# Projections of the first three batches as whole float32 matmuls in a planned transformer-block kernel

## The chip, the cores and the metric

The kernel runs on one core of a Trainium2 chip. A core has a matrix engine (TensorE, PE in the profile), a vector engine (VectorE, DVE), a scalar engine (ScalarE, ACT), a general engine (GpSimd, POOL) and a queue engine (SyncE, SP) that only issues transfers here. Each takes its instructions strictly in the order of its own queue and waits for the others through semaphores. PEld in the profile is TensorE loading stationary operands, which overlaps its matmuls. The metric is the time of one execution on the device in microseconds (us), the median over several runs.

## The reference, cut to what matters

For 16 batches of 512 tokens with 512 features, in float32:

```
n   = layernorm(x)                                    # no gain, no bias
h   = rmsnorm(n) * g_res @ W_in.T + b_in              # the projection, "a"
s   = scan over tokens of rmsnorm(ctx[:, :, :512]) * g_init   # decaying running sum
idx = clip(cumsum(boundary marks from mask) - 1)      # "plug": a row of s for each token
x   = x + h + s[idx]                                  # gather
y   = layernorm(x)
xr, xk = mix of y and y shifted by one token (mu_r, mu_k)
r   = sigmoid(xr @ W_r.T);  k = relu(xk @ W_k.T) ** 2
out = x + r * (k @ W_v.T)
```

So each batch has four matrix products of 512 x 512 x 512: a, k, r and v. The marks of a batch come from counting how many boundaries of the mask fall on each token; a running sum of the counts, cut at one, gives the index.

## The kernel before, in words

**Products in three passes.** A product in float32 is made of three products in the faster form fp32r: each operand is split into a high part (a copy to fp32r, `hi_w` for a weight) and a low part (the operand minus its high part, `lo_w`), and the list `QW` adds high by high, high by low and low by high. For one batch and 128 tokens that is 12 fp32r matmuls of 128 x 512, in three groups of four. The weights are kept whole in `wsa`, `wsk`, `wsr`, `wsv` (the transfers' target, two halves each) and split in `wha`, `wla` and so on.

**The projection.** Before the projection the weight W_in is scaled: `pm` (four plain float32 matmuls of 128 x 512 with `gmean`) makes the mean that the layernorm takes off, and `wsa<-wsa,small,pm` on VectorE folds gain and mean into the weight, a chunk at a time. Thus the raw x can be projected, and the scale of the norm (`rs`) is applied when the result `pa` is added to x (`a_end`). The operand has x with features on partitions. For batches 0 to 2 (`BY_PE`) x is loaded as it lies and turned by TensorE against the identity in `consts` into four buffers `tx` (`turn_x`); ScalarE copies each to its high part `xh` and VectorE makes the low part (`split_x`). For later batches a turned copy (`raw`) is loaded from memory. Batch 0 runs its projection chunk by chunk over four results at once (`a_first`), the others result by result (`a_mm`).

**The rest of a batch.** ScalarE squares the context rows `cx` and VectorE scales and scans them, with one carry product `pc` on TensorE; SP writes the scan to memory (`dr`); POOL gathers its rows by `plug` and adds them to x. VectorE takes the statistics, POOL a power, VectorE or ScalarE makes y; TensorE turns y (`tr`), ScalarE and VectorE mix it (`pv`, `m`), and k, r and v follow. `plugs(b0, n)` makes the index for batch 0 alone and then for groups of batches: `count` on TensorE, `marks` on VectorE, one matmul with `tri`, `index` on VectorE.

**The planner.** No line fixes the order of the instructions. Each piece of work is given with `add` (engines that may do it and a cost, what it reads and writes, a due time) and `Plan.order` deals the pieces to the engines by lateness, engine by engine; then each engine's queue stands fixed in that order. `START` and `PERIOD` set the order of TensorE's stages, `SHIFT` moves the due times of a stage by some microseconds, `ONLY` gives a stage's shared work to VectorE (0) or POOL (1), `ON_ACT`, `KR_DVE` and `Y_DVE` say which engine makes some statistics, squares and y, and `SLOTS` counts the buffers of each kind; `ps` and `tr` are eight banks of PSUM. `WARM` puts filler matmuls on `ones` (128 x 128) ahead of a stage, and `HEAT` at the start; their results are not used. Transfers from SP are tied to what TensorE is planned to have finished by then. `InOrder` records every operation at one line, L300, so that the profile's groups differ by tile.

Of the kernel before, what the change touches and what calls it, by code (L numbers as in the profile page):

```python
# [11 lines left out]
F32 = mybir.dt.float32  # L12
# [277 lines left out]
class InOrder:  # L290
# [27 lines left out]
PASS = 0.935  # L318
PERIOD = lambda i: (("a", i + 1), ("k", i))
TAT = {3: (0, 1, 2, 3)}  # L320
TAT_OF = {0: {0: (0, 1, 2, 3)}, 1: {0: (0, 1, 2, 3)}, 2: {0: (0, 1, 2, 3)}, 3: {0: (0, 1), 2: (2, 3)}, 4: {0: (0, 1), 2: (2, 3)}}
# [3 lines left out]
HEAT = 8  # L325
SHIFT = {
    ("a", 0): 2.1,
    ("gather", 0): 23.8,
    ("k", 0): 2.0,
    ("load", 0): -10.1,  # L330
    ("mix_k", 0): 5.2,
    ("mix_r", 0): -10.7,
    ("norm2", 0): -17.9,
    ("plugs", 0): -30.6,
    ("rv", 0): 1.3,
    ("scan", 0): -7.2,
    ("sq", 0): -19.5,
    ("stat1", 0): -7.7,
    ("store", 0): 1.6,
    ("wk", 0): -5.2,  # L340
    ("wv", 0): -6.2,
    ("a", 1): 10.4,
    ("bias", 1): 2.6,
    ("gather", 1): 3.0,
    ("k", 1): 4.0,
    ("mix_k", 1): -1.5,
    ("mix_r", 1): -3.9,
    ("norm2", 1): -3.6,
    ("plugs", 1): 0.3,
    ("rv", 1): 12.6,  # L350
    ("split_x", 1): -7.5,
    ("sq", 1): -9.3,
    ("stat1", 1): 0.2,
    ("a", 2): 1.0,
    ("bias", 2): 53.6,
    ("gather", 2): -18.5,
    ("load", 2): 5.1,
    ("mix_k", 2): 1.2,
    ("mix_r", 2): 4.1,
    ("norm2", 2): 6.6,  # L360
    ("rv", 2): -0.4,
    ("scan", 2): 0.4,
    ("split_x", 2): -5.3,
    ("sq", 2): 30.1,
    ("stat1", 2): -1.6,
    ("store", 2): -50.4,
    ("a", 3): 8.2,
    ("bias", 3): -12.0,
    ("gather", 3): -1.8,
    ("k", 3): -3.2,  # L370
    ("load", 3): -3.1,
    ("mix_r", 3): -1.7,
    ("norm2", 3): 10.1,
    ("split_x", 3): 9.0,
    ("sq", 3): 2.7,
    ("stat1", 3): -16.2,
    ("store", 3): 9.3,
    ("a", 4): 13.9,
    ("bias", 4): -18.4,
    ("gather", 4): 11.9,  # L380
    ("k", 4): 4.9,
    ("load", 4): 16.5,
    ("mix_k", 4): 0.0,
    ("mix_r", 4): -47.3,
    ("norm2", 4): -4.5,
    ("plugs", 4): 4.7,
    ("rv", 4): -2.0,
    ("split_x", 4): -0.3,
    ("sq", 4): 2.2,
    ("stat1", 4): 2.5,  # L390
    ("store", 4): -10.4,
# [3 lines left out]
ONLY = {  # L395
    ("rv", 0): 0,
    ("k", 2): 0,
    ("wr", 0): 0,
    ("k", 3): 1,
    ("mix_r", 0): 0,  # L400
    ("split_x", 3): 0,
    ("bias", 1): 0,
    ("wk", 0): 1,
    ("mix_r", 2): 0,
    ("rv", 3): 0,
    ("mix_k", 0): 1,
    ("wv", 0): 0,
    ("wv", 1): 0,
    ("mix_k", 3): 1,
    ("rv", 2): 0,  # L410
    ("wk", 3): 1,
    ("bias", 3): 0,
    ("wr", 2): 0,
    ("wr", 3): 1,
    ("mix_k", 2): 1,
    ("split_x", 2): 0,
    ("wv", 2): 0,
# [3 lines left out]
WARM = {  # L421
    ("k", 1, 0): 1,
    ("x", 2): 32,
    ("a", 3, 0): 15,
    ("r", 0, 0): 14,
    ("a", 2, 1): 7,
    ("a", 0, 0): 29,
    ("x", 0): 1,
    ("v", 0, 0): 10,
    ("x", 1): 1,  # L430
}
TIE = 5.0
KR_DVE = (1, 3, 4, 5, 10, 11, 15)
# [4 lines left out]
RAW_IN = {2: ("op", "raw")}  # L438
CX_IN = {}
NLATE = 4  # L440
NWHOLE = 2
Y_DVE = (0, 1, 2, 3)
# [5 lines left out]
LOADS = ["raw2"]  # L448
B_DUE, P_DUE = 3.31, 83.3
START = [("x", 0), ("a", 0), ("a", 1), ("x", 1), ("x", 2), ("a", 2), ("k", 0), ("t", 0)]  # L450
T0 = 14.3
ON_ACT = (0, 1, 3, 4, 5, 6, 9, 10, 11, 13, 15)
# [3 lines left out]
def block_kernel(  # L456
# [88 lines left out]
    LO = ((DVE, 0.61), (POOL, 1.26))  # L545

# [94 lines left out]

    def split_x(b, c):
        if b in BY_PE:
            n, t = f"xh{b}_{c}", f"tx{b}_{c}"
            add((ACT, 0.52), lambda e: e.copy(S[n][:, 0], S[t]), K(t, *J), K(n, 0), new={n: OP}, early=40)
            add((DVE, 0.6), lambda e: e.tensor_tensor(S[n][:, 1], S[t], S[n][:, 0].bitcast(F32), ALU.subtract),
                K(t, *J) + K(n, 0), K(n, 1))
            return
# [136 lines left out]

    def a_mm(b, j, due, kind=PS):
        n = f"pa{b}_{j}"
        sl = slice(j * P, (j + 1) * P)
        new = warm(("a", b, j), {n: kind}, due)
        for k, (q, w) in enumerate(QW):  # L790
# [8 lines left out]
    def a_first():  # L799

        ns = [f"pa0_{j}" for j in J]
        new = warm(("a", 0, 0), {n: TRP for n in ns}, due["a", 0, 0])
        for k, (q, w) in enumerate(QW):
# [217 lines left out]
    def plugs(b0, n):  # L1021
        cp = f"cp{b0}"
        cnt = lambda: S[cp][:, : n * NJ].rearrange("p (b j) -> p b j", j=NJ)
        pb = lambda: S[cp][:, n * NJ :]
        for b in range(b0, b0 + n):
# [7 lines left out]
            def count(e, b=b, oh=oh):  # L1033
# [5 lines left out]
                new=None if b > b0 else {cp: (("ps", "tr"), [P, n * (NJ + 1)], F32)})  # L1039

        def marks_1(e):

            bm = S[f"bm{b0}"] = spool.tile([P, 1, NJ], F16, tag="bm", name=f"bm{b0}")
            run = S[f"run{b0}"] = spool.tile([P, 1, NJ], F32, tag="pf", name=f"run{b0}")
            for j in J:
                if j:
                    e.tensor_scalar(run[:, 0, j : j + 1], cnt()[:, 0, j : j + 1], 1.0, run[:, 0, j - 1 : j], ALU.min, ALU.add)
                else:
                    e.tensor_scalar(run[:, 0, 0:1], cnt()[:, 0, 0:1], 1.0, None, ALU.min)
            e.tensor_copy(bm[:, 0, NJ - 1 : NJ], run[:, 0, NJ - 1 : NJ])  # L1050
# [27 lines left out]
    for what, b in START:  # L1078
        if b < NB and (what != "x" or b in BY_PE):
            for j in J:  # L1080
                slot((what, b, j), 0.43 if what in "tx" else 3 * PASS)
# [254 lines left out]
```

## Time and profile before

| what | value |
|---|---|
| median of 3 runs | 809.89 us (809.76 to 810.18) |
| the profiled execution's own time | 808.87 us |
| its span, first to last instruction | 807.1 us |
| mean granted TensorE clock | 0.994 |
| TensorE busy | 788.4 us (98%) |
| VectorE, ScalarE, GpSimd busy | 594.3, 486.0, 453.1 us |
| TensorE's first projection matmul | at 18.27 us |
| first matmul of r of batch 0 | at 83.96 us |
| moved by DMA | 134.69 MB, mean 167 GB/s |

A group of the profile reads: line, engine, operation, result<-operands (buffer numbers left out), sizes, count; then busy time and mean duration of one in ns; then the engine's idle time just before these instructions, with what ended most of it. In an answer in order of time the two first numbers are start and duration in us, and the bracket holds the idle time before and what ended it. Matmuls are pipelined, so the duration of one (about 400 ns) is longer than the time from one to the next; a group of four fp32r matmuls of 128 x 512 begins 0.93 us after the one before it. A plain float32 matmul stands as two records.

### The profile page before, as it was taken

The page shows a single profiled execution, that of the slowest core. Times are in us where ns is not written, and L with a number is a line of the kernel's source. Part 1 is how long each engine was busy: PE and PEld are TensorE (multiplying, and loading weights), DVE is VectorE, ACT ScalarE, POOL GpSimd, SP SyncE. Part 2 cuts the span into 40 slices and gives each one's busy share as a digit, 9 for nine tenths or more (in the row PEclk, how much of TensorE's full clock was granted, in tenths as well). Part 3 has the DMA queues.
Part 4 walks back from the last instruction along what each step waited for, and adds up shares of the span by engine and source line. Part 5 has one row for each costly group of instructions (what it writes and reads, how often), then busy time and mean ns, then how long its engine had stood idle before and what let it go on. Part 6 is the DMA issues. An engine that isn't in the chain of part 4 may idle for free. (4 is left out here: it accounts for less than half of the span.)

```text
span 807.1 us, 11158 instructions
## 1 busy us (share of the span) xinstructions
PE 788.4 (98%) x3627; PEld 628.2 (78%) x3627; DVE 594.3 (74%) x1323; ACT 486.0 (60%) x950; POOL 453.1 (56%) x374
## 2 busy tenths in 40 slices
PE   7998999999999999999999999999999999999997
PEld 4776877878787888888788888878788888888885
DVE  6899798989789696785857679685866949464432
ACT  6937496655483767467566756457675664655540
POOL 2843766574767656567665556537856554661220
PEclk8999999999999999999999999999999999999999
DMA  9867586895775777667665766756786674430011
GB/s 327 270 95 262 104 220 170 288 220 160 144 234 147 179 199 206 157 209 145 212 140 171 220 157 209 157 162 152 184 234 157 209 138 171 73 89 0 9 45 52
DMA packets 52554, 134.69 MB, mean 167 GB/s; under 512 B 4752, under 2 KB 5264, under 8 KB 50576
## 3 DMA queue, kind: packets, MB, share of 16 engines
q1 hardware_dynamic: 35744, 102.39, 37.3%
q0 software_dynamic: 16608, 31.46, 24.2%
q8 instruction: 28, 0.46, 0.2%
q14 instruction: 30, 0.25, 0.1%
q10 hardware_dynamic: 144, 0.13, 0.0%
HBM read 85.73 MB, written 33.55 MB: 148 GB/s over the span
## 5 line engine op out<-in xcount | busy, mean ns | idle before, releaser
L300 POOL TENSOR_TENSOR m<-pv,m 128x512 fp32r<-128x512 f32 x86 | 120.9, 1414 | 121.3 <-ACT m L300 59.7
L300 PE MATMUL pa<-wha,xh 128*128 128x512 f32 x512 | 136.7, 404 | 5.8 <-DVE x L300 2.0
L300 PE MATMUL pw<-whv,ka 128*128 128x512 f32 x512 | 139.0, 398 | 0.0
L300 POOL DMA_INDIRECT x<-dr,plug x64 | 113.2, 1769 | 45.3 <-issue 17.0
L300 PE MATMUL pr<-whr,m 128*128 128x512 f32 x512 | 138.4, 397 | 0.0
L300 PE MATMUL pk<-m,whk 128*128 128x512 f32 x512 | 133.8, 396 | 0.6 <-DVE x L300 0.6
L300 ACT ACTIVATE pv<-tr,om 128x384 f32<-128x384 f32 (+1 forms) x256 | 100.8, 485 | 52.4 <-PE tr L300 28.5
L300 DVE SCALAR_TENSOR_TENSOR pv<-tr,small,pv 128x511 f32<-128x511 f32 x128 | 94.9, 741 | 38.7 <-ACT pv L300 37.9
L300 PEld LDWEIGHTS pa<-wha,xh 128*128 128x128 f32 x512 | 96.9, 191 | 31.9 <-DVE x L300 2.8
L300 PEld LDWEIGHTS pk<-m,whk 128*128 128x128 f32 x512 | 95.6, 188 | 24.8 <-DVE x L300 1.0
L300 PEld LDWEIGHTS pr<-whr,m 128*128 128x128 f32 x512 | 95.5, 188 | 23.0 <-DVE kr L300 0.4
L300 PEld LDWEIGHTS pw<-whv,ka 128*128 128x128 f32 x512 | 95.0, 188 | 21.8
L300 ACT CAST m<-pv 128x512 fp32r<-128x512 f32 x128 | 76.1, 642 | 37.1 <-DVE pv L300 31.8
L300 ACT ACTIVATE sg<-pr 128x512 f32<-128x512 f32 x64 | 38.1, 598 | 95.6 <-PE pr L300 88.6
L300 DVE TENSOR_TENSOR ka<-kr,ka 128x512 fp32r<-128x512 f32 x48 | 35.9, 749 | 76.3 <-ACT ka L300 76.2
L300 DVE TENSOR_TENSOR sg<-pw,sg 128x512 f32<-128x512 f32 (+1 forms) x65 | 43.9, 676 | 41.5 <-PE pw L300 41.5
L300 ACT ACTIVATE junk<-cx 128x1024 bf16<-128x1024 f32 x64 | 67.5, 1055 | 6.7 <-DMA cx<-cx 6.1
L300 PE MATMUL pa<-wla,xh 128*128 128x512 f32 x256 | 71.2, 401 | 0.3 <-POOL wla L300 0.3
L300 ACT ACTIVATE y<-x,r 128x512 f32<-128x512 f32 x48 | 38.9, 814 | 53.7 <-DVE r L300 37.4
L300 PE MATMUL pw<-wlv,ka 128*128 128x512 f32 x256 | 70.4, 397 | 0.0
L300 PE MATMUL pr<-wlr,m 128*128 128x512 f32 x256 | 70.3, 396 | 0.0
L300 PE MATMUL pk<-m,wlk 128*128 128x512 f32 x256 | 69.9, 396 | 0.0
(116 smaller groups left out, 1238.9 us busy)
## 6 DMA issues: line engine op xcount, KB each, us to landing
cx<-cx SPq DMA_DIRECT2D x64, 512.0 KB
dr<-cx SPq DMA_DIRECT2D x64, 256.0 KB
out<-x SPq DMA_DIRECT2D x31, 512.0 KB
x<-x SPq DMA_DIRECT2D x15, 1024.0 KB
x<-bc POOLq DMA_DIRECT2D x14, 1024.0 KB
raw<-xT SPq DMA_DIRECT2D x26, 512.0 KB
wsa<-winT SPq DMA_DIRECT2D x2, 512.0 KB
x<-x SPq DMA_DIRECT2D x4, 256.0 KB
```

Of the source, the lines that this page charges most:

```text
L300: r = self._tc.keep_in_program_order(op(*args, **kwargs))
```

## The change

For batches 0 to 2 (`A_WHOLE`) the projection takes x and the scaled W_in unsplit, as plain float32 matmuls: four for each 128 tokens in place of twelve fp32r ones. Their turned x is copied out of PSUM once, to `xt` (ScalarE or VectorE), and not split. All batches' projections now go result by result (`ROWS_FIRST`). W_in is still split, for the batches from 3 on. The transfers at the start have a new order (`FIRST`): one part of batch 0's context, the small constants, x of batch 0, `consts`, W_in, then the other parts of the context with the bias and gain rows between; x, context of batch 1 follow ahead of x of batch 2 and W_k. The marks write only the last running sum to fp16, the running sum of each group is kept in float32, and the index is made inside the PSUM buffer `cp`, which grows for it, and written to `plug` by the operation that cuts it. The planner's settings (`SHIFT`, `ONLY`, `WARM`, `START` and others) have new values, and so each engine's order is new.

```diff
 PASS = 0.935
+WHOLE = 0.86
-TAT_OF = {0: {0: (0, 1, 2, 3)}, 1: {0: (0, 1, 2, 3)}, 2: {0: (0, 1, 2, 3)}, 3: {0: (0, 1), 2: (2, 3)}, 4: {0: (0, 1), 2: (2, 3)}}
+TAT_OF = {
+    0: {1: (0, 1), 3: (2, 3)},
+    2: {0: (0, 1, 2, 3)},
+    1: {1: (0, 1), 3: (2, 3)},
...
-HEAT = 8
+HEAT = 10
 SHIFT = {
...
 ONLY = {
...
+    ("bias", 0): 1,
+    ("bias", 1): 1,
...
-WARM = {
-    ("k", 1, 0): 1,
-    ("x", 2): 32,
-    ("a", 3, 0): 15,
-    ("r", 0, 0): 14,
-    ("a", 2, 1): 7,
-    ("a", 0, 0): 29,
-    ("x", 0): 1,
-    ("v", 0, 0): 10,
-    ("x", 1): 1,
-}
+WARM = {("r", 0, 0): 7, ("x", 2): 8, ("t", 1): 23, ("a", 2, 0): 36}
-KR_DVE = (1, 3, 4, 5, 10, 11, 15)
+KR_DVE = (3, 4, 5, 6, 10, 12, 13, 14, 15)
-RAW_IN = {2: ("op", "raw")}
-CX_IN = {}
-NLATE = 4
+RAW_IN = {3: ("raw", "op")}
+CX_IN = {1: ("cx", "op")}
+NLATE = 3
 NWHOLE = 2
-Y_DVE = (0, 1, 2, 3)
+FIRST = ["cx0_2", "small", "x0", "consts", "wa", "cx0_0", "cx0_3", "b", "cx0_1", "g"]
+ROWS_FIRST = True
+Y_DVE = (0, 3)
+A_WHOLE = (0, 1, 2)
-LOADS = ["raw2"]
-B_DUE, P_DUE = 3.31, 83.3
-START = [("x", 0), ("a", 0), ("a", 1), ("x", 1), ("x", 2), ("a", 2), ("k", 0), ("t", 0)]
-T0 = 14.3
-ON_ACT = (0, 1, 3, 4, 5, 6, 9, 10, 11, 13, 15)
+LOADS = ["raw2", "x1", "cx1"]
+B_DUE, P_DUE = 1.76, 1.15
+START = [("a", 0), ("x", 1), ("x", 0), ("a", 1), ("a", 2), ("x", 2), ("t", 0), ("k", 0)]
+T0 = 12.88
+ON_ACT = (2, 3, 4, 7, 9, 10, 12, 13)
...
+    CP = ((ACT, 0.52), (DVE, 0.6))
...
+    def xt(b, c):
+
+        return S[f"xt{b}_{c // 2}" if b in BY_PE else f"raw{b}_{c // 2}"][:, c % 2]
+
     def split_x(b, c):
+        if b in A_WHOLE:
+            if b in BY_PE:
+                n, t = f"xt{b}_{c // 2}", f"tx{b}_{c}"
+                add(CP, lambda e: copy(e, S[n][:, c % 2], S[t]), K(t, *J) + (K(n, "a") if c % 2 else []),
+                    K(n, c % 2) + ([] if c % 2 else K(n, "a")), new=None if c % 2 else {n: STAGE}, early=40)
+            return
...
+    def XT(b, c):
+        return K(f"xt{b}_{c // 2}", c % 2) if b in BY_PE else K(f"raw{b}_{c // 2}")
+
     def a_mm(b, j, due, kind=PS):
...
+        if b in A_WHOLE:
+            for c in range(NC):
+                add((PE, WHOLE), lambda e, c=c: e.matmul(S[n], xt(b, c)[:, sl], st("a", c), start=(c == 0), stop=(c == NC - 1)),
+                    XT(b, c) + K(f"wsa{c // 2}", c % 2), K(n), new=None if c else new, due=due + c * WHOLE, early=AHEAD)
+            return
...
-        pb = lambda: S[cp][:, n * NJ :]
+        pb = lambda: S[cp][:, n * NJ : n * NJ + n]
+        pf = lambda: S[cp][:, n * NJ + n :].rearrange("p (b j) -> p b j", j=NJ)
...
+                    e.scalar_tensor_tensor(run()[:, :, j], cnt()[:, :, j], 1.0, run()[:, :, j - 1], ALU.min, ALU.add)
...
         def index(e):
-            pf = spool.tile([P, n, NJ], F32, tag="pf", name=f"pf{b0}")
-            e.tensor_tensor(pf, S[f"run{b0}" if n == 1 else f"bm{b0}"], pb().unsqueeze(2).broadcast_to([P, n, NJ]), ALU.add)
-            e.tensor_scalar(pf, pf, -1.0, 0.0, ALU.add, ALU.max)
-            e.tensor_copy(plug[:, b0 : b0 + n], pf)
+            e.tensor_tensor(pf(), run(), pb().unsqueeze(2).broadcast_to([P, n, NJ]), ALU.add)
+            e.tensor_scalar(plug[:, b0 : b0 + n], pf(), -1.0, 0.0, ALU.add, ALU.max)
...
+    for k, what in enumerate(FIRST):
+        load_first(what, 0.05 * k - 9.5)
...
-        if b == 0:
+        if b == 0 and not ROWS_FIRST:
             a_first()
         for j in J:
-            if b:
-                a_mm(b, j, due["a", b, j], PST if b == 1 else PS)
+            if b or ROWS_FIRST:
+                a_mm(b, j, due["a", b, j], PST if b < 2 else PS)
             a_end(b, j)
```

## The prediction, made before the changed kernel was run

> **What bounds the kernel now.** I read the page's totals first, then TensorE's instructions in order of time, then a table of stretches cut at the moments at which the granted clock changes, and last the order of each engine's instructions in the changed kernel. The page (busy time, clock in 40 slices, and one group):
>
> ```profile
> span 807.1 us, 11158 instructions
> PE 788.4 (98%) x3627; PEld 628.2 (78%) x3627; DVE 594.3 (74%) x1323; ACT 486.0 (60%) x950; POOL 453.1 (56%) x374
> PEclk8999999999999999999999999999999999999999
> L300 PE MATMUL pa<-wha,xh 128*128 128x512 f32 x512 | 136.7, 404 | 5.8 <-DVE x L300 2.0
> ```
>
> TensorE sets the time, so the change is worth what it does to TensorE's own queue: work added, holes and slow clock removed. The holes lie in the first 84 us. A table of stretches gives TensorE 0.68 us idle from 83.96 to 200 us and 2.7 us from 200 to 780; the last 5 us are the tail after the last matmul. TensorE in order of time (start, duration, wait ended by):
>
> ```profile
> 5.28 3.65 PE L300 MATMUL pm<-wsa,gmean 128*128 128x512 f32 x8
> 9.15 2.56 PE L300 MATMUL tx<-consts,x 128*128 128x128 f32 x16 [0.22 <-DMA x<-x]
> 14.39 2.68 PE L300 MATMUL pa<-ones 128*128 128x128 f16 x29 [0.50 <-DVE pf L300]
> 18.27 5.64 PE L300 MATMUL pa<-wha,xh 128*128 128x512 f32 x16 [1.21 <-ACT wha L300]
> 37.07 1.92 PE L300 MATMUL tx<-consts,x 128*128 128x128 f32 x16
> 47.45 1.20 PE L300 MATMUL pa<-wha,xh 128*128 128x512 f32 x4 [1.60 <-DVE xh L300]
> 65.82 1.72 PE L300 MATMUL pa<-wha,xh 128*128 128x512 f32 x4 [2.01 <-DVE x L300]
> 83.96 1.18 PE L300 MATMUL pr<-whr,m 128*128 128x512 f32 x4
> ```
>
> The first projection starts at 18.27 us, the first pr at 83.96. The stretches (after the colon: the stretch's length, PE busy, PEld, DVE, ACT, POOL, then clock, DMA share, GB/s):
>
> ```profile
> 4.84:8.25 3.41, 3.35 (x19) 1.69 (x18) 1.30 (x9) 0.30 (x1) 1.55 (x5) 1.00 0.91 234
> 8.25:11.66 3.41, 3.17 (x22) 1.86 (x21) 2.42 (x8) 2.02 (x6) 0.05 (x1) 1.00 1.04 384
> 11.66:15.08 3.42, 0.98 (x19) 0.76 (x17) 3.02 (x13) 3.39 (x10) 0.56 (x1) 1.00 1.02 417
> 15.08:18.49 3.41, 2.20 (x21) 1.93 (x19) 3.41 (x8) 3.41 (x8) 1.30 (x3) 0.50 1.04 422
> 18.49:21.90 3.41, 3.41 (x9) 2.60 (x10) 2.96 (x6) 3.38 (x8) 2.67 (x3) 0.50 1.04 395
> 62.86:66.28 3.42, 1.41 (x7) 0.85 (x6) 3.42 (x8) 3.34 (x8) 2.65 (x3) 1.00 0.99 345
> 66.28:69.69 3.41, 3.41 (x10) 2.65 (x9) 3.19 (x6) 3.41 (x8) 2.35 (x2) 0.50 1.02 391
> ```
>
> After a stretch with 0.98 or 1.41 us of work the clock is half; after one with 3.41 it is whole again; 2.20 did not restore it.
>
> From 18.27 to 83.96, 65.7 us, needed work is 36 groups of four projection matmuls at 0.933 us (a group begins every 0.933 us in the dense part), 33.6; two sets of transposes at 1.9, 3.8; two pc at 0.86, 1.7; tr 1.6; k of batch 0, 12 x 0.933, 11.2; cp 0.4: together 52.3. Filler matmuls on ones take 3.0 (1.78 for 32, 0.37 for 7, 0.75 for 14). The other 10.4 are lost: 1.8 and 1.7 to half clock (18.27 to 21.90, 66.28 to 69.69), 5.0 to waits (0.3, 0.5, 1.6, 2.0, 0.6), the rest to small gaps.
>
> **The change, part by part.**
>
> *Whole projections.* For batches 0 to 2, 48 plain float32 matmuls replace 36 groups. The nearest row is pm, the same form: its eight half-matmuls begin 0.43 us apart, so 0.86 for one. That is 48 x 0.86 = 41.3 against 33.6: **+7.7 us** on TensorE, all on the path. A rule speaks against the change more strongly: the Trainium skill, "FP8 and Floating Point Precision", section "TensorE Precision Notes", gives true float32 four passes through the array. Four of this trace's fp32r matmuls are 0.933, so 44.8 and +11.2, by which the forecast would be 3.5 us later. I take pm's row, which is the operation itself.
>
> *Removed beside it.* VectorE loses 12 low parts of x at 0.68 (8.2 us) and, by the new owners of work, six additions of the bias (4.1); ScalarE's copies of x fall from 12 to 9, VectorE taking three. The split of Win remains, with all four low parts now on VectorE (2.7) but due only before batch 3's projections, which stand at 144 us in the trace: hidden by 60 us. This matters because the waits of 1.6 and 2.0 us above ended on VectorE, which works 20.03 of the 20.40 us between 45.85 and 66.25.
>
> *Loads and the first matmul.* SP now issues cx0's third part, small, four parts of x0, consts, the two halves of Win, then cx0's others with the bias row among them, g, x1, cx1, x2 and wk. Summing GB/s by microsecond, the trace has moved 1.84 MB by 8.4 us, 2.37 by 9.7 and 2.89 by 11.1; consts, whose last byte went at 6.0, was used at 6.46. So x0 and consts (1.84 MB) are there at 8.9, the halves of Win at 10.2 and 11.6. TensorE heats (ten matmuls, 1.34 to 5.3), does pcum and stands from 5.6 to 8.9: that stretch, 4.84 to 8.25, holds 0.8 us of work, so I expect half clock from 8.25. Transposes take 1.9 whole, 3.8 half. The next stretch is busy for 2.76 of 3.41, between 2.20 that did not restore the clock and 3.41 that did; I take restored, being nearer. Then 1.38 us' worth is done by 11.66, the rest by 12.2; pm (3.44) and the counts (0.24) end at 15.9; scaling a chunk of Win (0.74) and its hops make the first projection **16.9**, 1.4 earlier. Ends: 15.6 if x0's slow spell at 6 to 8 us (143 and 203 GB/s) doesn't return, 18.6 if the clock waits for 15.08. A second rule bears on this: the skill's "TensorE: Matmul & The Clock Gate", "Part 4: PE-mode transpose", says that transposes don't count as busy for the gate. In the trace the stretch 8.25 to 11.66 holds 0.5 us of pm and otherwise transposes, and the clock stayed whole after it; so they hold the clock. That they restore it, no row shows. By the rule the first projection is at 18.6 and the forecast 1.7 later.
>
> *From there to pr.* Needed 52.3 + 7.7 = 60.0; fillers 8 + 36 + 7 = 51 at 0.0555, 2.8: 62.8, hence pr at 79.7 with no wait at all. I followed the queues with the trace's durations. pc0: VectorE stands at the result of row 1 (the eighth matmul, 23.8) with the whole scan of cx0 queued behind; seven operations later it is done at 28.9, TensorE asks at 32.5. First transpose of y: on POOL four bias additions for x0 and four for x1 (1.28 each; the last waits for ScalarE's statistics of x1's last row, behind two copies of x, until about 33.7), two low parts of wk and two powers stand before the first gather, so it issues at 39.7 to 41.4 and lands about 44.6 (in the trace some 3.2 after the issue ends). VectorE comes to its statistics at 46.8, behind the result of a matmul that ends at 46.0, and y0 is ready at 50.6; TensorE arrives at 51.4, after 36 fillers. Slack 0.8 there, 2 at the gather. y1 to y3 (52.7, 56.3, 57.5) meet 53.9, 57.7, 59.0. k's m is ready at 62.9 against 64.3; wr, loaded ahead of the scan's writes now, has its last low part at 75.8. So none appears late, but such walks miss small things: between 0 and the trace's 5.0 I allow **1.0**, nearer zero because VectorE is relieved. pr then starts at **80.7, 3.3 earlier**.
>
> *After pr.* Fillers 23 (1.3) against 10 + 15 + 1 (1.4): even. v needs whv, whose copies stand on ScalarE behind relu, square and copy of all four k parts (82.5 + 2.2 = 84.7); TensorE asks at 87.8. The gathers of batch 1 wait for the index after k, 76.8, against 78.44 in the trace. Marks and index: still seven VectorE operations for a group of batches, one fewer for batch 0 (0.17), with tr buffers held no longer; nothing, since TensorE's cp stand inside k. On batches 1 to 3 the new owners move eight y from VectorE to ScalarE; TensorE idled 0.7 us there, so there is little to win and perhaps 1.5 to lose; I take nothing.
>
> **Sum**: +7.7 - 1.4 - 0.2 (fillers) - 10.4 + 1.0 = -3.3. The profiled execution is 808.87, its span 807.1: span 803.8, execution 805.6. The median of the runs is 809.89, 1.0 above that execution: **806.6**.
>
> **The rivals.** *Cold start*: half clock until 15.08, first projection at 18.6 and perhaps a second slow stretch: +1.7 to +3, 808.3 to 809.6. For it: 2.76 is not 3.41, and the start of the stretches may move between runs. Against: fillers then shrink into waits. *Late y*: before the first gather POOL now has eight bias additions, where the trace has two and three low parts of Win; if that gather is late, TensorE stands before the first transpose of y and cannot go round it. The hole at 63.81 cost itself (2.0) and 1.7 of half clock. This ends slower once y0 is 3.3 us past 51.4, as 3.3 + 1.7 eat the gain and pass 0.2%: 811.6 to 813.5. Against: slack of 2 at the gather. *More gain*: x0 arrives without its slow spell, no waits: -5.6, 804.3. For it: VectorE's 12 us. *Float32 dearer than pm's row* (the rule's 0.93): 810.1; against it pc, the same form, whose 0.86 the next group's start confirms.
>
> **How the numbers follow.** 0.2% is 1.6 us, about what a measurement of this kernel can tell from no change: faster is under 808.3, slower over 811.5. Likeliest, 806.6, own range 805 to 808.2: 0.55. More gain 0.15. Cold start 0.12 and dearer float32 0.03, both the same. Late y 0.15, slower. So faster 0.70, same 0.15, slower 0.15. For 8 in 10 the range takes the likeliest's and the two same cases and most of more gain, and leaves out late y: 804 to 811.
>
> **What would show it.** First pa at 16 to 18, in pairs 0.43 us apart; half clock around 8.3 to 11.7 and nowhere after 22; no wait before tr of y0; pr at about 80.7; TensorE's busy time up by some 4 to 5 us while the span falls. It is wrong if pm's 0.86 doesn't hold for pa, if TensorE stands before tr, or if idle after pr grows by over 2 us.

## The result, and the profile after

The changed kernel takes 812.45 us (median of 10 runs, 810.66 to 814.24), the kernel before, run beside it, 809.80 us. The ratio is 1.0032 (95% interval 1.0020 to 1.0045): slower by 0.32%, some 2.6 us. The forecast was 806.6, in a range of 804 to 811: wrong in sign.

The profiled execution of the changed kernel took 814.24 us, the slowest of its ten and 1.8 above their median; that of the kernel before lies 0.9 under its own. So the two spans differ by 5.4 us, of which about 2.7 is the change and the rest the draw of two executions. Where the draw sits is seen at the end of this section.

The page of the changed kernel:

```profile
span 812.5 us, 10981 instructions
PE 792.3 (98%) x3545; PEld 616.5 (76%) x3545; DVE 587.5 (72%) x1315; ACT 486.3 (60%) x941; POOL 456.8 (56%) x377
PEclk8999999999999999999999999999999999999999
```

TensorE is busy 3.9 us longer, as more work on it should show, but the span grew too. TensorE's instructions in order of time (start, duration, and the wait before it with what ended it):

```profile
6.69 0.18 PE L300 MATMUL pcum<-lh,small 128*128 128x48 f16 x1
10.08 3.65 PE L300 MATMUL tx<-consts,x 128*128 128x128 f32 x16 [3.20 <-DMA consts<-consts_d]
13.52 3.95 PE L300 MATMUL pm<-wsa,gmean 128*128 128x512 f32 x6
19.42 7.99 PE L300 MATMUL pa<-wsa,xt 128*128 128x512 f32 x18 [0.51 <-DVE sq L300]
35.87 7.03 PE L300 MATMUL pa<-wsa,xt 128*128 128x512 f32 x16
42.74 0.61 PE L300 MATMUL tx<-ones 128*128 128x128 f16 x8
51.86 2.17 PE L300 MATMUL pa<-ones 128*128 128x128 f16 x36
55.60 0.63 PE L300 MATMUL tr<-consts,y 128*128 128x128 f32 x4 [1.57 <-DVE y L300]
58.76 0.66 PE L300 MATMUL tr<-consts,y 128*128 128x128 f32 x4 [0.81 <-DVE y L300]
70.60 4.09 PE L300 MATMUL pk<-m,whk 128*128 128x512 f32 x16 [0.84 <-DVE x L300]
86.69 1.17 PE L300 MATMUL pr<-whr,m 128*128 128x512 f32 x4
```

Three things are to be seen. The first transposes wait 3.20 us for `consts` and then take 3.65, the half-clock duration. The 16 records from 35.87 to 42.74 (8 float32 matmuls) are 6.87 us, 0.86 each, as forecast. And there are waits of 1.57, 0.81 and 0.84 us before y's transposes and k. The stretches of the first line of trouble (length, then PE, PEld, DVE, ACT, POOL busy, clock, DMA share, GB/s):

```profile
5.70:9.12 3.42, 0.48 (x11) 0.33 (x10) 2.89 (x16) 0.23 (x1) 1.01 (x4) 1.00 0.94 335
9.12:12.53 3.41, 2.45 (x12) 2.48 (x13) 1.81 (x10) 2.93 (x9) 2.28 (x5) 0.50 1.05 409
12.53:15.95 3.42, 3.42 (x9) 2.00 (x8) 2.21 (x7) 2.40 (x5) 0.47 (x1) 0.50 1.04 402
15.95:19.36 3.41, 2.72 (x11) 0.95 (x9) 1.64 (x8) 2.50 (x6) 0.08 (x1) 1.00 1.00 378
```

The clock is half from 9.12 to 15.95: after a stretch with 0.48 us of work, and for two stretches, since 2.45 us in the first of them did not bring it back. From there on it is whole to the end; the two slow spells of the kernel before (15.1 to 21.9, 66.3 to 69.7) are gone. The stretches follow each other every 3.41 us, as in the kernel before, but they begin at other moments: one at 9.12 here, one at 8.25 there.

| profiled, us | before | predicted | after | after minus predicted |
|---|---|---|---|---|
| first projection starts | 18.27 | 16.9 | 19.42 | +2.5 |
| from there to the first r matmul | 65.69 | 63.8 | 67.27 | +3.5 |
| from there to the end of the span | 723.14 | 723.1 | 725.81 | +2.7 |

The first two rows put the first r matmul at 86.69 against 83.96, 2.73 later, which is the 2.65 between the medians. The third row is the draw: four of the kernels below keep every queue after that point as it is here, and they take 723.7 to 724.2; two that keep the queues of the kernel before take 724.3 and 724.5. So TensorE's idle time after the first r matmul, 2.6 us more here than in the trace before, is by these kernels the draw and not a cost of the change; 'even after r' was right, and what is to be explained is the 6 us between 80.7, the forecast for the first r matmul, and 86.69.

### The profile page after: what moved, and what is told of

Same layout as the page of the kernel before. It is cut to its first block, busy times and chain, and to the rows that moved or that the text cites. A ratio compares the mean times of both kernels' runs of the same rounds, so it can differ in the third digit from the quotient of the medians.

```text
span 812.5 us, 10981 instructions
## 1 busy us (share of the span) xinstructions
PE 792.3 (98%) x3545; PEld 616.5 (76%) x3545; DVE 587.5 (72%) x1315; ACT 486.3 (60%) x941; POOL 456.8 (56%) x377
## 4 chain that ended last, share of the span: by engine, by line
PE 74%; DVE 9%; POOL 5%; DMA 4%; ACT 4%; issue 4%; SPq 0%; POOLq 0%; DVEq 0%; ACTq 0%
PE pr L300 18%; PE pk L300 18%; PE pa L300 17%; PE pw L300 16%; PE tr L300 3%; DVE pv L300 2%; POOL m L300 2%; DVE cx L300 2%; DVE x L300 1%; POOL x L300 1%; PE pc L300 1%; ACT kr L300 1%; DMA x<-dr,plug 1%; DMA out<-x 1%; DMA cx<-cx 1%
## 5 line engine op out<-in xcount | busy, mean ns | idle before, releaser
L300 POOL TENSOR_TENSOR m<-pv,m 128x512 fp32r<-128x512 f32 x86 | 118.4, 1405 | 102.3 <-ACT m L300 49.9
L300 DVE SCALAR_TENSOR_TENSOR pv<-tr,small,pv 128x511 f32<-128x511 f32 x128 | 95.0, 742 | 42.7 <-ACT pv L300 42.5
L300 PE MATMUL pa<-wha,xh 128*128 128x512 f32 x416 | 109.4, 397 | 1.8 <-ACT kr L300 1.7
L300 PEld LDWEIGHTS pa<-wha,xh 128*128 128x128 f32 x416 | 77.4, 188 | 22.7 <-ACT kr L300 3.1
L300 DVE TENSOR_TENSOR ka<-kr,ka 128x512 fp32r<-128x512 f32 x52 | 38.6, 744 | 74.1 <-ACT ka L300 74.1
L300 ACT ACTIVATE y<-x,r 128x512 f32<-128x512 f32 x56 | 45.2, 813 | 54.8 <-DVE r L300 26.8
L300 POOL TENSOR_TENSOR r<-r,mhalf 128x1 f32<-128x1 f32 x64 | 39.6, 619 | 60.8 <-DVE r L300 46.7
```

The source lines that it names most:

```text
L300: r = self._tc.keep_in_program_order(op(*args, **kwargs))
```

## The experiments

Where only single instructions of the changed kernel are added or moved, its median can be read off the start of r to about 1 us; *hot_apart3* is the exception. ("In its place" in an expectation means that no other instruction changes its place in its queue.) Where the planner has dealt the queues anew, much more changes than the edit says; this is told each time.

### The start: fillers, or consts first

The first projection came 2.5 us later than forecast. Two causes stand beside each other in the trace, late `consts` and half clock. Two kernels each remove one. *hot* puts fillers into the hole:

```diff
 HEAT = 10
+HOT = 56
...
             def fn(e, j=j):
+                for _ in range(HOT if b == j == 0 else 0):
+                    e.matmul(S[ns[0]][:, :P], ones, ones, start=True, stop=True)
                 for c in range(NC):
                     e.transpose(S[ns[c]][:, j * P : (j + 1) * P], S[f"x{b}"][:, j, c * P : (c + 1) * P], ident)
```

> The changed kernel with 56 filler matmuls ahead of the first transposes of x0 (3.1 us at 0.0555), while TensorE waits for consts; every other instruction keeps its place. Theory 'cold start is a term of the sum': the clock stays whole, the transposes take 1.9 instead of 3.6 us and the mean product loses its half-clock part, first projection at 17.0 instead of 19.42, first r matmul near 84.3, total 2.4 us under the changed kernel (812.45), 810.0. Rival 'the gather sets it': the first projection moves as much, but batch 0's gathered rows land when the scan lets them, so the wait before the transposes of y grows from 1.57 to about 4 us and the total falls by less than 0.5 us, 812 to 812.5.

*consts* takes piece 6 (the transfer of `consts`) to the place behind piece 1 (`small`) after the planner has fixed the orders; the same lines, with other numbers, serve the later kernels:

```diff
-    for start, e, p, take in plan.order():
+    out_of = plan.order()
+    for n, m in MOVE:
+        i = next(k for k, o in enumerate(out_of) if o[2].n == n)
+        o = out_of.pop(i)
+        out_of.insert(next(k for k, q in enumerate(out_of) if q[2].n == m) + 1, o)
+    for start, e, p, take in out_of:
...
+MOVE = [(6, 1)]
```

> The changed kernel with consts issued ahead of the four parts of x0, no fillers, every other instruction in its place. TensorE then turns each row of x0 as it lands, from about 7.6, and the hole of 3.5 us is cut to 1 us and small ones. Theory 'the clock, not the wait, was the price': the stretch 5.7 to 9.1 still holds under 2.2 us of work, the clock is half at least until the next stretch ends, and the first projection comes at 17.5 to 18.5, total 811. Rival 'the wait for consts was the price': first projection at 16.2 or earlier and the total as with the fillers, 809.3.

Measured: *hot* 809.31 us, ratio to before 0.9994 (0.9985 to 1.0004); *consts* 809.39, 0.9995 (0.9987 to 1.0003). Both are 3.1 us faster than the changed kernel. TensorE in *hot*:

```profile
6.55 3.29 PE L300 MATMUL tx<-ones 128*128 128x128 f16 x56
9.67 1.92 PE L300 MATMUL tx<-consts,x 128*128 128x128 f32 x16
11.43 2.74 PE L300 MATMUL pm<-wsa,gmean 128*128 128x512 f32 x6
16.12 7.99 PE L300 MATMUL pa<-wsa,xt 128*128 128x512 f32 x18 [0.51 <-DVE sq L300]
```

and in *consts*:

```profile
7.62 3.62 PE L300 MATMUL tx<-consts,x 128*128 128x128 f32 x16 [0.79 <-DMA x<-x]
11.22 2.85 PE L300 MATMUL pm<-wsa,gmean 128*128 128x512 f32 x6
16.22 7.99 PE L300 MATMUL pa<-wsa,xt 128*128 128x512 f32 x18 [0.51 <-DVE sq L300]
```

With late consts and a whole clock the projection starts at 16.12, with early consts and half clock in the transposes (3.62) at 16.22. So neither alone costs anything: the loss of 3.2 us is their product, transposes that start late and then run at half speed, with the mean product behind them slowed as well (3.95 us for six records, 2.74 in *hot*). My expectation for *hot* had the place right and 0.9 us too little. In *consts* the theory I wrote first, that the clock alone was the price, fell.

The two remedies together (in *best*, below, which changes more) bring it to 16.36, no lower: its mean product starts at 11.21 after a wait of 0.80 although the transposes are done by 10.4. What ends that wait the profile doesn't settle: it names an operation of VectorE that is long over, so probably the W_in transfer, which is not shown. One thing stays open: of the changed kernel's ten executions one had a mean clock of 0.999, too high for 6.8 us at half clock, and still took 812.06. No trace of it was kept.

### Is a bridged hole worth its half clock in the kernel before?

36 fillers into the hole of the kernel before at 11.7 to 13.7, ahead of the marks' last product:

```diff
 HEAT = 8
+HOT = 36
...
-        add((PE, 0.05), lambda e: e.matmul(pb(), tri, S[f"bm{b0}"][:, :, NJ - 1], start=True, stop=True),
+        def base(e):
+            if not b0:
+                hot2 = pools["ps"].tile([P, D], F32, tag="ps3", name="hot2")
+                for _ in range(HOT):
+                    e.matmul(hot2[:, :P], ones, ones, start=True, stop=True)
+            e.matmul(pb(), tri, S[f"bm{b0}"][:, :, NJ - 1], start=True, stop=True)
+
+        add((PE, 0.05), base,
```

> The kernel before with 36 filler matmuls (2.0 us) in the hole at 11.7 to 13.7 before the last product of the marks, every instruction else in its place. Theory 'a bridged hole is worth its half clock': the clock stays whole from 15.1 to 21.9, where 1.8 us went, total 808.3. Rival 'the operands set the pace there': the matmuls run faster into the waits for the low parts of W_in and of x, and the total is within 0.5 of 810.1.

Measured 810.70 us, ratio 1.0008 (0.9996 to 1.0020): nothing gained. Its TensorE, and the clock by the microsecond (length, PE busy, clock, DMA share, GB/s):

```profile
12.50 2.17 PE L300 MATMUL hot<-ones 128*128 128x128 f16 x36
15.24 1.79 PE L300 MATMUL pa<-ones 128*128 128x128 f16 x29 [0.49 <-DVE pf L300]
19.12 5.59 PE L300 MATMUL pa<-wha,xh 128*128 128x512 f32 x16 [2.09 <-ACT wha L300]
```

```profile
16.00:17.00 1.00, 1.00 (x19) 1.00 1.08 426
17.00:18.00 1.00, 0.03 (x1) 1.00 1.00 410
18.00:19.00 1.00, 0.00 (x0) 1.00 1.10 446
19.00:20.00 1.00, 0.88 (x3) 0.71 0.88 340
20.00:21.00 1.00, 1.00 (x4) 0.50 1.04 381
```

This execution stands 0.84 us behind the one of before from x0's landing on (transposes at 9.99 against 9.15). Against that the old fillers, now at whole clock, take 1.79 in place of 2.68, so the wait for the high part of W_in is 2.09 where it was 1.21, and this hole halves the clock from 19.4 on. The hole was moved, not bridged. The second theory was the nearer one, 0.1 us outside what it allowed, and by another way than it said. Two of the twelve executions had a mean clock of 0.999 and took 811.35 and 810.51, so nothing on record shows that a whole clock would gain there.

### The wait before y: earlier gather

In the changed kernel the first gather is issued at 43.46, and VectorE stands for its rows:

```profile
43.46 1.73 POOL L300 DMA_INDIRECT x<-dr,plug  x1 [0.19 <-issue]
```

```profile
51.63 0.69 DVE L300 BATCH_NORM_STATS2 sb<-x 128x6 f32<-128x512 f32 x1 [2.12 <-DMA x<-dr,plug]
54.92 0.54 DVE L300 TENSOR_SCALAR y<-x,r 128x512 f32<-128x512 f32 x1
```

The issue ends at 45.19 and the rows are there at 51.6: 6.4 us, where the forecast took 3.2. The first test issues the gather two pieces earlier (133 is the gather, 198 the power for the context of batch 1, 156 a low part of W_k):

```diff
+MOVE = [(198, 133), (156, 198)]
```

> The changed kernel with the first gather of batch 0 two pieces earlier on GpSimd: ahead of the power for batch 1's context and of the second low part of W_k. Theory 'late y': it is issued at about 41.2 instead of 43.46, its rows land by 49, y0 is ready by 52.7 and the wait of 1.57 us before the first transposes of y is gone: first r matmul at 85.1 or earlier, total 1.6 us under the changed kernel, 810.9. Rival 'the transfers beside it set it': the gather issued earlier meets the four context loads of batch 2 in full and lands no earlier than 50.5; the wait stays over 1 us and the total is within 0.5 of 812.45.

Measured 813.50 us, ratio 1.0044 (1.0031 to 1.0056), a microsecond worse than the changed kernel. GpSimd and VectorE in it:

```profile
42.37 1.74 POOL L300 DMA_INDIRECT x<-dr,plug  x1 [1.88 <-DVE x L300]
49.24 1.88 POOL L300 DMA_INDIRECT x<-dr,plug  x1 [0.16 <-issue]
```

```profile
45.25 2.43 DVE L300 SCALAR_TENSOR_TENSOR cx<-cx,sq,bc 128x512 f32<-128x512 f32 x2 [1.82 <-POOL sq L300]
55.34 0.69 DVE L300 BATCH_NORM_STATS2 sb<-x 128x6 f32<-128x512 f32 x1 [0.99 <-DMA x<-dr,plug]
```

Both theories missed. GpSimd stood 1.88 us before the gather; the engine named had done its part, and in the program the gather waits only for transfers, the scan's writes to memory. So it could not go before about 42.4, only 1.1 us earlier than it did, and the power behind it then held up VectorE for 1.82. VectorE reached row 0's statistics at 52.01 without a wait for the rows. But the edit also put a low part of W_k between the two gathers, and the next low part behind it waited 1.36 for ScalarE; the second gather was issued at 49.24 in place of 46.66. Row 1's statistics stand ahead of y0 in VectorE's queue and began at 55.34, so the wait before the transposes of y grew to 2.73. The test therefore bounds one thing alone: what stood on GpSimd ahead of the first gather, the bias additions among it, made it at most 1.1 us late.

### The wait before y: loads held away from the gathers

What else shares the transfer engines? SP issues the four context loads of batch 2 (512 KB each) right behind the scan's writes, and W_r's halves after them. Four kernels on top of *hot* hold these back. Pieces 274 to 277 are the loads, 165 and 166 W_r, 288 to 291 ScalarE's squares of that context, 292 and 293 the two steps behind them on VectorE and GpSimd; the start planned for a transfer sets which matmul it waits for.

```diff
+MOVE = [(288, 285), (289, 288)]
+DELAY = {274: 12.0, 275: 12.0, 276: 12.0, 277: 12.0, 165: 12.0, 166: 12.0}
...
+        start += DELAY.get(p.n, 0.0)
```

> The changed kernel with the 56 fillers (809.31), and with the four context loads of batch 2 and the two halves of W_r held back until TensorE has passed a point some 7 us later, so that the first gathers have the transfer engines to themselves; ScalarE takes two copies of x2 ahead of the squares of that context, so that it doesn't stand in front of the late loads. Theory 'the gather shares the transfer engines': its rows land 3.2 us after the issue ends, as in the kernel before, in place of 6.1; y0 is ready by 49.5, the waits of 1.25 and 0.81 us before the transposes of y go, total 807.3. Rival 'VectorE's queue sets y0': the rows land earlier but the context's operations ahead in VectorE's queue keep y0 at 51; total within 0.5 of 809.3.

Measured 810.15 us, ratio 0.9995 (0.9985 to 1.0006). The delay did not do what I wrote: the loads were issued from 37.56 in place of 35.97, because the tie reaches only matmuls that the program has listed by then. That put more of them onto the gather: it is issued 0.45 us later than in *hot*, its rows land 1.7 us later (49.7 against 48.0), and the wait before y0 is 2.5 in place of 1.25. Behind that wait the clock is half from 55.1 to 58.5. An inconclusive kernel for the total, but a dose in the other direction. The next moves the loads in the listing too:

```diff
+MOVE = [(274, 247), (275, 274), (276, 275), (277, 276), (165, 277), (166, 165), (288, 166), (289, 288), (290, 289), (291, 290)]
+DELAY = {274: 14.0, 275: 14.0, 276: 14.0, 277: 14.0}
```

> As hot_clear, with the loads held back further: the four context loads of batch 2 and W_r are issued behind a matmul of the last result of batch 1, near 46 us, and not at 37.6; the four squares of that context follow on ScalarE. The first gathers then have the transfer engines nearly to themselves. Theory 'the gather shares the transfer engines': batch 0's first rows land about 45.2 (3.2 after the issue ends at 41.9) in place of 48.0, y0 is ready by 49.5, no wait before the transposes of y, first r matmul near 81, total 807.3. Rival 'the gather is slow by itself': the rows land after 47 again and the wait before the transposes stays over 1 us, total 809 to 810.

Measured 814.88 us, ratio 1.0069 (1.0047 to 1.0090). Its first gather, the transfer rate beside it (clock, DMA share and GB/s stand last), and VectorE:

```profile
40.25 1.73 POOL L300 DMA_INDIRECT x<-dr,plug  x1 [0.19 <-issue]
```

```profile
43.00:44.00 1.00, 1.00 0.73 117
44.00:45.00 1.00, 1.00 0.66 117
45.00:46.00 1.00, 1.00 0.00 0
```

```profile
46.24 0.68 DVE L300 BATCH_NORM_STATS2 sb<-x 128x6 f32<-128x512 f32 x1
49.51 0.54 DVE L300 TENSOR_SCALAR y<-x,r 128x512 f32<-128x512 f32 x1
58.89 0.15 DVE L300 TENSOR_SCALAR sq<-sq 128x1 f32<-128x1 f32 x1 [2.45 <-ACT junk L300]
```

Alone, the gather's rows have moved by 45.0, 3.0 us after its issue ends at 41.98, and y0 is ready at 49.5 to 50, as the forecast had it (50.6); TensorE transposes it without a wait. That the loads make the gather late is shown: beside them the same gather takes 6.1 to 7.4 us. How, the packets of *hot* tell, by queue (packets, MB, share of the 16 engines). The gathers are q0, SP's transfers q1; the first gather's issue ended at 41.89. From 44 to 45 us, from 45 to 46 us, and VectorE:

```profile
q1 hardware_dynamic: 157, 0.35, 96.7%
```

```profile
q1 hardware_dynamic: 126, 0.23, 61.0%
q0 software_dynamic: 47, 0.10, 52.0%
```

```profile
48.01 0.69 DVE L300 BATCH_NORM_STATS2 sb<-x 128x6 f32<-128x512 f32 x1 [1.79 <-DMA x<-dr,plug]
```

No packet of the gather moves before 45.0, 3.1 us after its issue ended; in *hot_apart* the first moves between 42.5 and 42.75, 0.5 to 0.8 after. From its first packet to its rows the gather takes 3.0 in *hot* and some 2.4 in *hot_apart*. So most of the delay is a late beginning and not a slower run; why its queue stands until the loads let up is open. But the total is 5.6 us above *hot*. The loads are late now, VectorE stands at 58.89 for a square of the late context, row 3's statistics are behind it, and TensorE waits there:

```profile
61.18 1.11 PE L300 MATMUL tr<-consts,y 128*128 128x128 f32 x4 [3.73 <-DVE y L300]
```

The clock is half from 60.3 to 67.2, so the eight transposes and 14 projection records from here on take 10.65 us where they take 7.56 in *hot*.

*best* has the same loads held back, with consts first and 16 fillers in place of 56:

> The changed kernel with consts ahead of x0, 16 fillers in the small hole that stays ahead of the first transposes, and the loads held back as in the last. Theory 'late consts and the clock hurt only together': either remedy alone brought the first projection to 16.1 to 16.2, so both bring it no lower than 15.5, and the total is that of the last kernel within 0.5, 807.0. Rival 'each has a price of its own': first projection at 14 or earlier, total 805 or less.

Measured 814.87 us, ratio 1.0060 (1.0040 to 1.0079), the time of *hot_apart*. On the start the first theory held (16.36); the total is far off, for the reason just seen (a wait of 4.87 at the same place). Two more kernels move the readers of the late context out of the way:

```diff
+MOVE = [(165, 325), (166, 165), (274, 166), (275, 274), (276, 275), (277, 276), (288, 173), (289, 288), (290, 424), (291, 290), (292, 60), (293, 292)]
+DELAY = {165: 20.0, 166: 20.0, 274: 20.0, 275: 20.0, 276: 20.0, 277: 20.0}
```

> The fillers, and the loads held back as in hot_apart, but W_r first and batch 2's context after it, both behind the fillers at 50.7; two squares of that context stand on ScalarE behind the high parts of W_r and two behind the operands of r, with VectorE's and GpSimd's operations on them moved to 75 us, so that no instruction that row 2 or 3 of y needs stands behind a late load. Theory 'the collision cost the two waits, and holding the loads back cost more only through the queues': y0 at 49.5, waits before the transposes of y under 0.5 us in all, first r matmul near 81, total 807.3. Rival 'what is held back returns elsewhere': the loads now collide with the third and fourth gather and with the bias transfer, y2 or y3 or the operands of k are late by 2 us or more, total 809 or more.

Measured 816.18 us, ratio 1.0088 (1.0062 to 1.0114). The waits before the transposes of y are 0.36 us in all, and TensorE then reaches k at 64.6, 1.5 us sooner than in *hot*, to stand there:

```profile
70.33 6.67 PE L300 MATMUL pk<-m,whk 128*128 128x512 f32 x16 [5.74 <-DVE x L300]
```

ScalarE makes k's operands behind two squares that wait for the context, then waits for buffers that the scan's writes of batch 1, queued behind those loads, have yet to free. The clock is half from 69.5 to 76.3, so the 16 records take 6.67 us where they take 4.10 in *hot*. Last, the context behind those writes, and all four squares behind r's operands:

```diff
+MOVE = [(165, 325), (166, 165), (274, 214), (275, 274), (276, 275), (277, 276), (288, 424), (289, 288), (290, 289), (291, 290), (292, 172), (293, 292)]
+DELAY = {165: 20.0, 166: 20.0}
```

> As hot_apart2 with the context loads of batch 2 behind the scan's writes of batch 1 (near 61 us), their squares on ScalarE behind the operands of r, where it stood idle from 71 to 76 us, and the operations on them after 77 us. Only W_r is left between the first gathers and those writes. Theory 'the bunched transfers cost the waits': y as in hot_apart2 (waits 0.4 in all), and k's first operands no longer behind late squares: pk at 64.6 to 65, first r matmul at 80.5 to 81, total 806.9. Rival 'what is held back returns elsewhere': the late context or the late W_r is awaited by the scan of batch 2, by v or by the operands of r; total 809 or more.

Measured 811.30 us, ratio 1.0017 (1.0010 to 1.0025), 2.0 above *hot*. y waits 0.4 in all, k 1.39 (it waited 0.84 in *hot*), the counts of the marks 1.2 between the matmuls of k, and, after r has started (at 83.38, 0.3 later than in *hot*), the transposes of batch 1's y 1.4. In all four kernels in which y was on time, *best* among them, what y won came back further on, or more. In three of them a good part of that is half clock behind the new hole, and none tried fillers there; *hot_apart3* has no such spell (mean clock 0.999) and still gained nothing. Four orders are not every order, but none took out the wait before y alone.

### One part alone

*b_whole* gives the kernel before the new projection (the functions `xt`, `split_x`, `a_mm` and `a_first` of the change) with its own settings, and the planner deals the queues anew; *b_marks* gives it the new marks and index, every other instruction in its place.

```diff
+WHOLE = 0.86
+A_WHOLE = (0, 1, 2)
```

> The kernel before with the unsplit projections of batches 0 to 2 alone (same settings, same transfers, same fillers, same marks); the planner deals the orders anew. By the recorded sum: +7.7 us for the float32 matmuls, less the holes that split x and W_in caused (waits of 1.2, 1.6 and 2.0 us and 1.7 us of half clock behind them, 6.5 in all): 811.0 against 809.8. If those holes are not caused by the split, the whole +7.7 shows: 817.5. If nearly all that was lost before the first r matmul goes (10.4), 807.1.

> The kernel before with the new marks and index in PSUM alone, every instruction else in its place. By the recorded sum nothing: within 0.5 us of 810.1. If the index of batch 0 (two operations at the end in place of three) or the kept tr buffer matters: 1 us either way.

*b_marks*: 810.23 us, ratio 1.0005 (0.9992 to 1.0018): no change beyond the noise, as the sum had it. *b_whole*: 814.03, ratio 1.0046 (1.0029 to 1.0064): +4.0 us, between the two ends. TensorE in it:

```profile
16.32 15.21 PE L300 MATMUL pa<-wsa,xt 128*128 128x512 f32 x32
66.41 4.56 PE L300 MATMUL pa<-wsa,xt 128*128 128x512 f32 x10 [1.33 <-DVE x L300]
73.34 5.50 PE L300 MATMUL pk<-m,whk 128*128 128x512 f32 x16 [2.37 <-DVE x L300]
```

The start gains 1.95 us (no high part of W_in to wait for) and the waits of 1.6 and 2.0 are gone, but waits of 1.33 and 2.37 have come in their place, and the clock is half for 3.4 us behind the second (this execution is the slowest of five, 2.7 above their median). In the medians the relief pays for about half of the 7.7 us of the float32 matmuls.

*hot_01* and *hot_0* have the fillers of *hot* and float32 for fewer batches (`(0, 1)` and `(0,)`), *wafirst* the transfers in the order of the kernel before. In all three the planner dealt the queues anew.

```diff
-A_WHOLE = (0, 1, 2)
+A_WHOLE = (0, 1)
```

> The changed kernel with the 56 fillers, float32 projections for batches 0 and 1 only; batch 2 is split as before and the planner deals the orders anew. Theory 'each float32 batch costs its matmuls': 16 at 0.865 against 12 groups at 0.933, 2.6 us less, total 806.7. Rival 'the relief of VectorE pays for it': four low parts at 0.68 and four high parts come back into the stretch in which y0 and the k operands are made, and the waits grow by as much; total 809 to 810.

> As the last, with batch 0 alone in float32. By the first theory 5.3 us less than with three, 804.0; by the rival 809 or more, since eight low parts (5.4 us of VectorE) come back before k of batch 0.

```diff
-FIRST = ["cx0_2", "small", "x0", "consts", "wa", "cx0_0", "cx0_3", "b", "cx0_1", "g"]
+FIRST = ["small", "wa", "consts", "x0", "g", "cx0_0", "cx0_1", "cx0_2", "cx0_3", "b"]
```

> The changed kernel with the first transfers in the order of the kernel before (small, W_in, consts, x0, g, the four context parts, b); the planner deals the engines' orders anew as far as batch 2. Theory 'the order of the transfers spoilt the start': the mean product runs at 5.3 as before and bridges the wait for x0, the clock stays whole, and as the projection no longer waits for the high part of W_in it starts at about 14 instead of 19.42; the context comes as early as before and the first gather issues at about 37 to 39; first r matmul at 82 or earlier, total 4 to 6 us under the changed kernel, 807 to 808.5. Rival 'VectorE is the bound of the start': the scaled W_in and the result of the first row come no sooner because VectorE is busy from 11 us on; first projection at 17 or later or as much new waiting behind it; total 811 to 813.

Measured 825.37, 824.54 and 822.10 us in this order (ratios 1.0180, 1.0179 and 1.0138, each to about 0.002): no expected total came true, save that *hot_0*'s rival allowed anything from 809 up. *hot_01* waits 5.2 us before y and 5.1 before k, *hot_0* 2.4 for the split of x before a transpose and 2.3 before a projection, and has its pc 4.9 us late for no reason that the profile names. *wafirst* does start its projection at 13.62, as the theory said, yet its first gather is issued at 42.38, and k waits 6.4. These kernels price neither float32 nor the order of the transfers; they show what dealing anew costs with settings that were not made for it: some 10 to 16 us here.

## Why the prediction was wrong, point by point

Two steps carry the miss of 6.0 us at the first r matmul: when consts is there (the first projection, +2.5), and the allowance for waits and gaps from there on, 4.5 in place of 1.0 (+3.5), of which the two waits before y, behind gathers that landed late, are 2.4.

- **Whole projections, +7.7: right.** 0.86 each in the trace. The 0.93 that I weighed against it did not come: 'FP8 and Floating Point Precision', 'TensorE Precision Notes', in the Trainium skill, gives float32 four passes, and I took the 0.233 us from one fp32r matmul to the next for a pass. Four equal passes in 0.86 would be 0.215 each, so the price of a pass was too high; the number of passes no run tests. The net cost alone, +4.0 in *b_whole*, is smaller because the start and two waits give way.
- **First projection at 16.9: failed, +2.5.** The first step to fail is 'x0 and consts are there at 8.9': the transposes waited for consts until 10.08. The bytes were not late: summed as in the forecast, 1.84 MB had moved by 8.6 us and 2.41 by 10.0. But W_in's halves were issued from 4.13 and two more parts of the context from 5.70, and by the same sums about 0.6 MB of them went ahead of the last of consts (an estimate). The forecast counted bytes as if transfers ended in the order of their issue. From this follows the second failure, 'restored, being nearer': the stretch that should have held 2.76 us of work held 2.45, and the clock stayed half for another 3.4 us. Whether 2.76 would have restored it no run shows; 2.57 did not (*hot_apart*, 60.34 to 63.75), 3.29 did (*best*, 62.33 to 65.74). *hot* and *consts* show that either alone is harmless (16.12, 16.22). The cold-start rival had this mechanism and mis-sized it: 18.6 for 19.42.
- **No wait before y, slack 2 at the gather: failed.** The gather was to issue at 39.7 to 41.4; where the start is on time (*hot*, *hot_apart*) it issues at 40.2, so that walk was good. The failing step is 'lands some 3.2 after the issue ends': true alone (3.0 in *hot_apart*), 6.1 in *hot* and 6.4 here, beside loads that I had put on SP's queue and not on the transfer engines. Nor was 3.2 a safe reading of the trace. There only gathers moved from 40 us on, and the one that VectorE waited for, issued until 39.87, took 5.1:

```profile
44.93 0.69 DVE L300 BATCH_NORM_STATS2 sb<-x 128x6 f32<-128x512 f32 x1 [0.24 <-DMA x<-dr,plug]
```

  With 0.84 at k there are 3.2 us of waits, and by difference another 1.3 of small gaps: 4.5 for an allowance of 1.0.
- **The late-y rival** had the right place and a price that holds the result (811.6 to 813.5), but not the cause. GpSimd's queue held the gather back by 1.1 us at most (*gather*), y0 came 1.6 after TensorE and not 3.3, and the clock held: the stretch with that hole (53.50 to 56.91, counted on from 15.95) has 1.84 us of work. That the time fell in this rival's range is luck: the cold start made up the difference.
- **What was lost before, 10.4, goes, 1.0 comes back: mis-sized.** The half clock of 66 us and the waits of 1.6 and 2.0 did go. Half clock at the start and waits at y and k came instead. The same in *b_whole*: a wait was taken away and the next operand set the pace.
- **Even after r, marks at nothing: right**, by *b_marks* and by the 723.7 to 724.2 us of the kernels with the same queues.
- **Rules of the Trainium skill.** 'TensorE: Matmul & The Clock Gate', 'Part 4: PE-mode transpose', says that transposes don't count as busy for the gate, and by it the first projection was 18.6. It came later still, but not by the rule: in *consts* the clock is half from about 7.9 to 11.3, with nothing on TensorE up to 11.2 except transposes, and whole after:

```profile
10.50:11.00 0.50, 0.50 (x4) 0.50 1.06 410
11.00:11.50 0.50, 0.50 (x3) 0.70 1.08 422
11.50:12.00 0.50, 0.50 (x2) 1.00 1.06 422
```

  So these float32 transposes do restore the clock when they fill the stretch, and the measurement decides against the rule. What was missing in the changed kernel was work in the stretch: 2.45 us in 3.41 was not enough.

What is shown: the cold start is 3.1 of the lost microseconds, and without it the changed kernel is within the measurement of the one before (0.9994). That the loads make the gather, and so y, late is shown too; that this costs the total its 2 us is not, since no order that avoids it was faster. No version tried beats both kernels clearly.

## What to carry to other kernels

A transfer's time from issue to landing is a property of what runs beside it: before a duration is taken from a trace, look at what the transfer engines moved in that stretch, and list what the change puts there, transfers issued later included. When operands are relieved, look for the operand that is next (in *b_whole* the next ones took back about half), and take a hole at the start together with the clock of what follows it, since a late start and a half clock multiply. In a planned kernel, move single pieces under a frozen order to test a cause, and look at what the move puts behind it (*gather*); a changed setting deals everything anew and can cost more than what it tests.

## What the runs showed of the hardware that I had not expected

- A hole of about 2 us can be enough to halve the clock: 2.09 us before 19.12 in *b_hot* (half from 19.4), 2.5 us before 53.71 in *hot_clear* (half from 55.1). 1.57 us before 55.60 in the changed kernel was not. Counted by stretches of 3.41 us, those with 1.32 (*b_hot*) and 1.36 us of work (*hot_clear*) were followed by half clock, and that with 1.84 (the changed kernel) was not. At half clock 2.56 us of work (*hot_apart2*, 69.48 to 72.89) did not bring the whole clock back, and 3.29 (*best*) did.
- A gather that adds into its target takes 3.0 us from the end of its issue with the engines to itself (*hot_apart*, 117 GB/s), and 6.1 to 7.4 behind plain loads, with 190 to 370 GB/s moved in all. In *hot* none of its packets moves in the first 3.1 of these, while some 350 packets of the loads do. The highest rate is not the longest wait: *hot_clear* has 7.4 with 188 to 277 GB/s.
- Filling a hole can open the next one: fillers run at whole clock are done 0.9 us sooner, and the engine then waits longer for the same operand.
